# Layer 0's attention sums: the residual on VectorE reads them from PSUM, without ScalarE's copy in SBUF

## The chip, the core and the metric

The kernel runs on one core of a Trainium2 chip. The core has four compute engines and a DMA issuer, each with its own queue of instructions: TensorE (PE, matrix products; PEld is its loading of weights), VectorE (DVE), ScalarE (ACT), GpSimd (POOL) and SyncE (SP, which issues DMAs). [...] TensorE writes its sums to PSUM, a small memory that VectorE and ScalarE also read; everything else lies in SBUF. The metric is the device time of one execution in microseconds (us). All data are float32 unless said otherwise.

## The reference, cut to what matters

Sixteen graphs of 1024 nodes with 256 features pass through four layers, each of the form

```
h = relu(layernorm(x))
x = x + layer(h, adj)
```

Layer 0 is graph attention with its softmax over axis 1, and an ELU at the end:

```
h = input @ W                          # 1024 x 256
e = leaky_relu(f1[:, :, None] + f2[:, None, :], 0.2)
attention = softmax(where(adj > 0, e, NEG_BIG), axis=1)
return elu(attention @ h)
```

Layer 1 is the same with the softmax over the last axis, layer 2 sums over neighbours, divides by the degree and ends in a ReLU, and layer 3 is attention with four heads, a ReLU and a second normalisation. The change concerns only how `elu(s)` with `s = attention @ h` is added to x in layer 0.

## The kernel before, in words

A tile is 128 nodes (the partitions) by 256 features, so a graph has NT = 8 tiles. The kernel computes elu(s) as max(s, 0) + min(exp(s), 1) - 1; the constant -1 per layer is left out of x on the way (the normalisations subtract the mean, and two of them are put back in the row `beta3`, L521). So a tile's end is `x += min(exp(s), 1)` (L736) and `x += max(s, 0)` (L737), two VectorE instructions; L737 also sums the new x along the row into `after.sums`, which the next normalisation needs.

**Layer 0** (L742 to L795), per graph: eight projections (L686, ScalarE evicts them at L746); a row of exponentials sent to all partitions by way of DRAM (L711); eight tiles of attention weights `p` on VectorE (L769, L771), with column sums z by which ScalarE scales the rows of hs (L773); then eight output tiles. Each output tile is a sum of eight products (L759; sixteen matmul instructions, as a float32 product is issued as two) in a PSUM buffer of the pool `at_ps`, which has two buffers. The first EARLY = 2 tiles are summed while the weights are made; tiles 2 to 7 each take the buffer of the tile two before, when that one's last reader is done. Per tile, ScalarE reads the sums twice: `e = exp(s)` (L791) and the copy `v` (L793); then `residual(xs, i, v, after, e)` runs L736 and L737.

**What follows a pair of tiles.** After every second tile `Norm.pair` takes the sums, makes the negative mean `shift` (L635), and ScalarE makes `hn = relu(x + shift)` (L667) and the sum of squares (L640), from which GpSimd makes the inverse deviation (L592, L593). At the next pair `flip` has TensorE transpose hn into PSUM (L680), and ScalarE copies it to `ht` (L681), the input of the next layer's projection.

**Layer 1** ends in the same way, but its `e` and `v` are scaled by 1/z on ScalarE (L838, L840). **Layer 2** has v and no e (L891). Its sums and layer 3's lie in another pool, `hd_ps`. **Layer 3** makes weights p with VectorE (L929), 1278 ns each, and products of 64 weight columns (L942).

**What sets the order.** Each graph is a generator that yields the estimated us of what it has just put down; graph b is due at b x 120, and a loop at the end always goes on with the piece that is due next. So the late layers of one graph are written down between the early layers of the next. The framework then plans each engine's queue from this order, its own estimates of duration, and what is ready and which buffers are free in the plan; it also places all semaphores. Instructions passed to `later(...)` keep the written order on their engine. Among layer 0's outputs of graph b + 1 lie the end of layer 2 and the projection (L906) and first heads of layer 3 of graph b.

Of the kernel before, what the change touches and what calls it, by code (L numbers as in the profile page):

```python
# [8 lines left out]
F32 = mybir.dt.float32  # L9
# [5 lines left out]
P = 128  # L15
# [406 lines left out]
def tile_simple_stack(  # L422
# [11 lines left out]
    nc = tc.nc  # L434
    B, N, D = x.shape
# [32 lines left out]
    work = ctx.enter_context(tc.tile_pool(name="work", bufs=2))  # L468
# [214 lines left out]
    def project(norm, w, n, width):  # L683
        ps = mm_ps.tile([P, HALF], F32, tag="mm", name="ps_proj")
        for c in range(DC):
            nc.tensor.matmul(ps[:, :width], norm.ht[:, c, n * P : (n + 1) * P], w[:, c, :width], start=(c == 0), stop=(c == DC - 1))  # L686
        return ps

    def new_hs(name="hs"):
        return state.tile([P, NT, W3], F32, tag="hs", name=name, bufs=3)  # L690

    def spread(col, n, scales, name):

        k = n * NT
        ps = tr_ps.tile([P, P], F32, tag="tr", name="ps_col")
        nc.tensor.transpose(ps[:k, :], col, ident)
        all_rows = []  # L700
        for scale in scales:
            e = small.tile([H * NT, P], F32, tag="e_row", name="e_row", bufs=2)
            nc.scalar.activation(e[:k, :], ps[:k, :], AF.Exp, scale=scale)
            d = dram.tile([n, N], F32, tag=f"row_{name}", name="d_row", bufs=4)
            later(nc.sync.dma_start(d.rearrange("r (t p) -> (r t) p", p=P), e[:k, :]))
            all_rows += [d[r] for r in range(n)]
        return all_rows

    def everywhere(d, tag):
        row = work.tile([P, N], F32, tag=tag, name="row", bufs=2)  # L710
        later(nc.sync.dma_start(row, d.partition_broadcast(P)))  # L711
        return row

    def column(src, n):

        col = small.tile([P, H, NT], F32, tag="col", name="col", bufs=2)
        nc.vector.tensor_copy(col[:, :n, :], src.rearrange("p t n -> p n t"))
        return col[:, :n, :].rearrange("p n t -> p (n t)")

    def watch(b, layer, terms):  # L720
        k = b * 3 + layer
        nc.vector.tensor_reduce(top[:, k : k + 1], terms, axis=AX.XY, op=OP.max, apply_absolute_value=True)

    def weights(name):
        return work.tile([P, N], F32, tag="p", name=name, bufs=NT)

    def residual(xs, i, v, after, e=None):

        x = xs[:, i, :]
        if i % 2 == 0:  # L730
            if i == NT - 2:
                after.settle()
            after.flip()
            after.sums = small.tile([P, 2], F32, tag="sums", name="sums")
        if e is not None:
            nc.vector.scalar_tensor_tensor(x, e, 1.0, x, op0=OP.min, op1=OP.add)  # L736
        nc.vector.scalar_tensor_tensor(x, v, 0.0, x, op0=OP.max, op1=OP.add, accum_out=after.sums[:, i % 2 : i % 2 + 1])  # L737
        if i % 2:
            after.pair(xs, i // 2, after.sums)


    def layer0(b, xs, m, norm, after):  # L742
        hs = new_hs()
        for n in range(NT):
            ps = project(norm, wx[0], n, D + 2)
            nc.scalar.activation(hs[:, n, : D + 2], ps[:, : D + 2], AF.Copy, scale=norm.rs[n])  # L746
            m.step()
            yield 0.9
        mask = m.bytes
        row_a, row_b = [everywhere(d, "row") for d in spread(column(hs[:, :, D : D + 1], 1), 1, (1.0, S), "l0")]  # L750
        q = small.tile([P, NT], F32, tag="q", name="q")
        nc.scalar.activation(q, hs[:, :, D + 1], AF.Exp, scale=1.0 - S)
        watch(b, 0, hs[:, :, D : D + 2])
        yield 6.38
        ps_ = []
        early = [at_ps.tile([P, HALF], F32, tag="at", name="ps_o0") for _ in range(EARLY)]

        def product(ps, i, j):
            m = nc.tensor.matmul(  # L759
                ps[:, :D], ps_[j][:, i * P : (i + 1) * P], hs[:, j, :D], start=(j == 0), stop=(j == NT - 1)  # L760
            )
            if i < EARLY and j < 7:
                later(m)

        for j in range(NT):
            if m.raws:
                m.step(2)
            p = weights("p0")
            nc.vector.scalar_tensor_tensor(p, row_a, q[:, j : j + 1], row_b, op0=OP.mult, op1=OP.max)  # L769
            z = small.tile([P, 2], F32, tag="z", name="z", bufs=8)  # L770
            nc.vector.scalar_tensor_tensor(p, p, 1.0, mask[:, j, :], op0=OP.mult, op1=OP.mult, accum_out=z[:, 0:1])  # L771
            nc.vector.reciprocal(z[:, 1:2], z[:, 0:1])
            nc.scalar.activation(hs[:, j, :D], hs[:, j, :D], AF.Copy, scale=z[:, 1:2])  # L773
            ps_.append(p)
            if b == 0:
                gates.append(p)
            for i, ps in enumerate(early):
                if j:
                    product(ps, i, j - 1)
            yield 2.6  # L780
        for i, ps in enumerate(early):
            product(ps, i, NT - 1)
        for i in range(NT):
            if i < EARLY:
                ps = early[i]
            else:
                ps = at_ps.tile([P, HALF], F32, tag="at", name="ps_o0")
                for j in range(NT):
                    product(ps, i, j)
            e = work.tile([P, D], F32, tag="e", name="e")  # L790
            nc.scalar.activation(e, ps[:, :D], AF.Exp)  # L791
            v = work.tile([P, D], F32, tag="v", name="v")
            nc.scalar.copy(v, ps[:, :D])  # L793
            residual(xs, i, v, after, e)
            yield 3.9  # L795


# [208 lines left out]
    def graph(b):  # L1006
        xs = loaded.pop(b)
        m = masks.pop(b)
        norm = Norm()
        for g in range(NT // 2):  # L1010
            norm.pair(xs, g)
            m.step()
            yield 2.66
        for layer, inputs in ((layer0, (m,)), (layer1, (m.bytes,)), (layer2, ())):
            yield 2.36
            norm.settle()
            norm.flip()
            after = Norm(degrees(b) if layer is layer1 else None)
            yield from layer(b, xs, *inputs, norm, after)
            norm = after  # L1020
        yield 1.44
        norm.flip()
        res = state.tile([P, NT, H, HW], F32, tag="res", name="res", bufs=1)
        hs = yield from layer3(b, xs, m.bytes, norm, res)
        return tail(b, xs, hs, res)
# [49 lines left out]
    ps = tr_ps.tile([P, P], F32, tag="tr", name="ps_bad")  # L1075
# [64 lines left out]
```

## Time and profile before

Median of 3 runs: 2629.38 us (2628.99 to 2631.85). The profiled execution spans 2618.6 us, with a mean granted TensorE clock of 0.984.

| what | instructions | busy us | mean ns |
|---|---|---|---|
| L759 PE, products of layer 0 | 2048 | 495.6 | 387 |
| L791 ACT, e from PSUM | 128 | 48.6 | 380 |
| L793 ACT, v from PSUM | 128 | 47.2 | 368 |
| L736 DVE, x with e (layers 0 and 1) | 256 | 108.0 | 422 |
| L737 DVE, x with v (layers 0, 1 and 2) | 384 | 160.5 | 421 |
| L737 DVE, reading out the row sum | 384 | 31.1 | 81 |
| L667 ACT, hn in layers 0, 1 and 3's norms | 384 | 176.8 | 500 |
| L929 DVE, p of layer 3 | 512 | 632.9 | 1278 |

How to read the profile: a busy time is that of the engine's own instructions; idle time is put down to the instruction whose semaphore came last before the waiting one began. Instructions of different queues overlap, and neighbours on one queue overlap a little too, as one starts before the other's recorded end. A matmul's recorded duration is longer than its pace, since matmuls are pipelined: L759's follow each other every 0.215 us or so. In the time order a row such as "351.18 2.14 PEld L759 ... x10" merges ten instructions in a row; the first number is the start in us, the second what they took.

### The profile page before, as it was taken

Reading aid. Unit: us, or ns where it says so; the run is one execution under the profiler, and the core shown is the slowest. Engines: PE = TensorE matmul, PEld = TensorE weight load, DVE = VectorE, ACT = ScalarE, POOL = GpSimd, SP = SyncE. Lnnn points to the kernel's source line nnn. Section 1 sums busy time; section 2 is a strip of 40 time slices with the busy share of each in tenths; the row PEclk is TensorE's granted clock in tenths of the full one; section 3 lists DMA queues with packets and bytes.
Section 4 is the critical chain, followed back from the end, with each engine's and each line's share of the span. In section 5 each row is a group of like instructions: output and inputs, shape, how many; then the busy total and the mean of one; then the engine's idle time right before and its main releaser. Section 6 shows DMA issues by size and latency. Waiting matters only on the chain.

```text
span 2618.6 us, 62976 instructions
## 1 busy us (share of the span) xinstructions
PE 2473.6 (94%) x26194; PEld 2100.8 (80%) x26194; DVE 1965.5 (75%) x3815; ACT 1448.0 (55%) x4065; POOL 438.4 (17%) x454
## 2 busy tenths in 40 slices
PE   5899999999999999999999999999999999999985
PEld 4688788888878888788888878888888888878864
DVE  4357778787777877778787777977778787777858
ACT  4564755637565474755637565473755637555350
POOL 1020211203112030211202112030211203111021
PEclk7899999999999999999999999999999999999997
DMA  4531351616217161251616217161351616216021
GB/s 153 117 85 55 93 110 58 125 59 142 66 51 152 65 127 55 91 113 58 125 55 141 70 54 149 66 125 54 99 105 58 125 57 140 70 49 126 26 65 36
DMA packets 212633, 233.76 MB, mean 89 GB/s; under 512 B 10416, under 2 KB 161072, under 8 KB 212336
## 3 DMA queue, kind: packets, MB, share of 16 engines
q0 software_dynamic: 137728, 83.90, 19.4%
q1 hardware_dynamic: 74608, 145.73, 17.1%
q8 instruction: 208, 3.41, 0.5%
q14 instruction: 89, 0.73, 0.1%
HBM read 212.35 MB, written 17.24 MB: 88 GB/s over the span
## 4 chain that ended last, share of the span: by engine, by line
PE 51%; DVE 16%; ACT 15%; DMA 9%; issue 7%; POOL 2%; SPq 0%; DVEq 0%; POOLq 0%; ACTq 0%
PE ps_o L759 16%; PE ps_proj L686 11%; PE ps_o L942 11%; PE ps_o L883 6%; DVE p L929 5%; DVE p L822 4%; ACT hn L667 4%; DMA row<-d_row 3%; DMA raw<-in_adj_t 3%; ACT mask L575 2%; PE pt_h L680 2%; ACT unread L640 2%; PE ps_o L877 2%; PE ps_o L815 2%; POOL rs L593 2%
## 5 line engine op out<-in xcount | busy, mean ns | idle before, releaser
L929 DVE SCALAR_TENSOR_TENSOR p<-row,q,mask 128x1024 f32<-128x1024 f32 x512 | 632.9, 1278 | 60.8 <-PE ps_o L942 51.0
L942 PEld LDWEIGHTS ps_o<-hb,p 128*64 128x64 f32 x16384 | 506.9, 139 | 96.0 <-issue 44.7
L942 PE MATMUL ps_o<-hb,p 128*64 128x65 f32 x16384 | 544.7, 224 | 19.2 <-DVE p L929 6.1
L686 PE MATMUL ps_proj<-wx,ht 128*128 128x258 f32 (+2 forms) x2048 | 517.3, 392 | 6.5 <-ACT hs L746 5.0
L759 PE MATMUL ps_o<-hs,p 128*128 128x256 f32 x2048 | 495.6, 387 | 16.5 <-ACT hs L773 15.9
L815 PE MATMUL ps_o<-hs,p 128*128 128x257 f32 x2048 | 498.1, 390 | 13.0 <-ACT mask L575 7.4
L759 PEld LDWEIGHTS ps_o<-hs,p 128*128 128x128 f32 x2048 | 381.1, 193 | 70.2 <-ACT hs L773 21.5
L815 PEld LDWEIGHTS ps_o<-hs,p 128*128 128x128 f32 x2048 | 374.0, 191 | 69.3 <-ACT mask L575 7.6
L686 PEld LDWEIGHTS ps_proj<-wx,ht 128*128 128x128 f32 x2048 | 360.0, 190 | 85.7 <-ACT hs L746 16.0
L592 POOL TENSOR_SCALAR rs<-mv 128x4 f32<-128x4 f32 (+1 forms) x112 | 33.7, 301 | 1561.4 <-ACT unread L640 1546.8
L736 DVE SCALAR_TENSOR_TENSOR xs<-e,xs 128x256 f32<-128x256 f32 x256 | 108.0, 422 | 237.3 <-ACT e L791 164.0
L593 POOL TENSOR_TENSOR rs<-rs,neg_half 128x4 f32<-128x4 f32 (+2 forms) x144 | 257.3, 1790 | 10.7
L667 ACT ACTIVATE hn<-xs,shift 128x256 f32<-128x256 f32 x384 | 176.8, 500 | 128.3 <-DVE shift L635 126.7
L680 PE MATMUL pt_h<-ident,hn 128*128 128x128 f32 x1024 | 183.6, 285 | 37.9 <-ACT hn L667 36.5
L950 ACT ACTIVATE res<-ps_o 128x260 f32<-128x260 f32 x128 | 48.7, 381 | 298.6 <-PE ps_o L942 298.2
L883 PE MATMUL ps_o<-hi,adj 128*128 128x258 f32 x1024 | 201.2, 320 | 2.4 <-DMA adj<-in_adj 2.3
L680 PEld LDWEIGHTS pt_h<-ident,hn 128*128 128x128 f32 x1024 | 118.3, 141 | 105.6 <-ACT hn L667 85.8
L575 ACT ACTIVATE mask<-raw 128x512 uint8<-128x512 int32 x256 | 160.5, 627 | 71.8 <-DMA raw<-in_adj_t 70.6
L585 POOL DMA_DIRECT2D adj<-in_adj x128 | 114.5, 895 | 486.2 <-PE ps_o L883 452.8
L737 DVE SCALAR_TENSOR_TENSOR xs<-v,xs 128x256 f32<-128x256 f32 x384 | 160.5, 421 | 19.6 <-DVE xs L736 0.5
L769 DVE SCALAR_TENSOR_TENSOR p<-row,q 128x1024 f32<-128x1024 f32 x128 | 159.8, 1269 | 19.7 <-DMA row<-d_row 19.7
L883 PEld LDWEIGHTS ps_o<-hi,adj 128*128 128x128 f32 x1024 | 150.8, 190 | 18.3 <-DMA adj<-in_adj 4.8
(108 smaller groups left out, 3005.4 us busy)
## 6 DMA issues: line engine op xcount, KB each, us to landing
raw<-in_adj_t SPq DMA_DIRECT2D x256, 256.0 KB
adj<-in_adj POOLq DMA_DIRECT2D x128, 512.0 KB, 5.6
row<-d_row SPq DMA_DIRECT2D x112, 512.0 KB
xs<-in_x POOLq DMA_DIRECT2D x32, 512.0 KB, 7.8
out<-xs SPq DMA_DIRECT2D x32, 512.0 KB
wx<-in_w SPq DMA_DIRECT2D x3, 256.0 KB
d_row<-e_row SPq DMA_DIRECT2D x48, 4.0 KB
wts<-in_w_t SPq DMA_DIRECT2D x2, 256.0 KB
```

Source lines behind the costliest of these rows:

```text
L575: nc.scalar.activation(self.bytes[:, n, g * HALF : (g + 1) * HALF], raw, AF.Square, accum_out=squares[:, k : k + 1])
L593: nc.gpsimd.tensor_tensor(rs[:, :n], rs[:, :n], neg_half[:, :n], op=OP.pow)
L667: nc.scalar.activation(hn, xs[:, 2 * g + k, :], AF.Relu, scale=scale, bias=bias)
L680: nc.tensor.transpose(pt[:, c, k * P : (k + 1) * P], hn[:, c * P : (c + 1) * P], ident)
L686: nc.tensor.matmul(ps[:, :width], norm.ht[:, c, n * P : (n + 1) * P], w[:, c, :width], start=(c == 0), stop=(c == DC - 1))
L737: nc.vector.scalar_tensor_tensor(x, v, 0.0, x, op0=OP.max, op1=OP.add, accum_out=after.sums[:, i % 2 : i % 2 + 1])
L759: m = nc.tensor.matmul(ps[:, :D], ps_[j][:, i * P : (i + 1) * P], hs[:, j, :D], start=(j == 0), stop=(j == NT - 1))
L769: nc.vector.scalar_tensor_tensor(p, row_a, q[:, j : j + 1], row_b, op0=OP.mult, op1=OP.max)
L815: nc.tensor.matmul(ps[:, : D + 1], ps_[j][:, i * P : (i + 1) * P], hs[:, j, : D + 1], start=(j == 0), stop=(j == NT - 1))
L883: nc.tensor.matmul(ps[:, : D + 2], adj_n[j][:, i, :], h[:, i, : D + 2], start=False, stop=(h is lo and i == NT - 1), skip_group_check=True,)
L929: nc.vector.scalar_tensor_tensor(p, row, q[:, jj, h : h + 1], mask[:, jj, :], op0=OP.max, op1=OP.mult)
L942: nc.tensor.matmul(pss[g][part, k * HW : (k + 1) * HW], ps_[t][:, i * P : (i + 1) * P][:, part], hbv[:, j + t, h, :], start=(j == 0 and t ...
```

## The change

Layer 0's copy `v` is left out, with its SBUF tile, and `residual` is given the PSUM sums themselves. L737 in layer 0 thus reads x from SBUF and s from PSUM. L736 is as before, and so are layers 1 and 2, whose v is scaled. It is for taking one instruction per output tile, 128 in all, from ScalarE; the last reader of each PSUM buffer of layer 0 is now VectorE's L737 in place of ScalarE's L793.

```diff
             e = work.tile([P, D], F32, tag="e", name="e")
             nc.scalar.activation(e, ps[:, :D], AF.Exp)
-            v = work.tile([P, D], F32, tag="v", name="v")
-            nc.scalar.copy(v, ps[:, :D])
-            residual(xs, i, v, after, e)
+            residual(xs, i, ps[:, :D], after, e)
             yield 3.9
```

## The prediction

> **What bounds the kernel now.** I read the busy shares first, then the windows over one period of the pipeline, then the time order around the changed lines, and last the waits. Busy time of the whole run:
>
> ```profile
> PE 2473.6 (94%) x26194; PEld 2100.8 (80%) x26194; DVE 1965.5 (75%) x3815; ACT 1448.0 (55%) x4065; POOL 438.4 (17%) x454
> ```
>
> TensorE (PE) is nearly always busy, ScalarE (ACT) half the time. A share is a mean over stages, so here is one period of about 157 us, cut at the stages (layer 0's outputs of one graph run from 350 to 382 us):
>
> ```profile
> 350.00:357.80 7.80, 7.78 (x40) 6.12 (x39) 3.91 (x14) 7.32 (x26) 1.22 (x2) 1.00 0.33 62
> 357.80:382.00 24.20, 24.20 (x186) 20.46 (x186) 16.55 (x32) 11.14 (x36) 1.20 (x2) 1.00 0.23 77
> ...
> 430.00:470.00 40.00, 37.60 (x237) 30.38 (x237) 26.63 (x69) 34.26 (x91) 11.83 (x10) 1.00 0.22 67
> ```
>
> The columns after the length are busy us of PE, PEld (weight loads), DVE (VectorE), ACT, POOL. From 357.8 to 382 PE is full and ACT has 13 us to spare; from 430 to 470 ACT is the full engine, but no copy of L793 lies there. Only in the first 7.8 us is ACT tight (94%) where the change acts. Who waits for the copies and for their neighbours (us in total, times, longest):
>
> ```profile
> DVE xs L736 <- ACT e L791: 164.0, 80, 5.7
> ...
> ACT e L791 <- PE ps_o L759: 159.0, 66, 4.2
> ...
> PEld ps_o L759 <- ACT v L793: 0.7, 1, 0.7
> ```
>
> DVE's residual waits for the exponential e, and e for the matmuls. The copy v is hardly waited for: PE once for 0.7 us, and among the releasers of L737 stands v of layer 1 (L840, 0.4 us) but not v of L793. L737 finds v ready because L736 runs while v is copied.
>
> The time order at the start of the outputs, where the first two tiles come together because their sums were built early:
>
> ```profile
> 350.26 0.37 ACT L791 ACTIVATE e<-ps_o 128x256 f32<-128x256 f32 x1
> 350.52 0.36 ACT L793 COPY v<-ps_o 128x256 f32<-128x256 f32 x1
> 350.66 0.42 DVE L736 SCALAR_TENSOR_TENSOR xs<-e,xs 128x256 f32<-128x256 f32 x1 [1.24 <-ACT e L791]
> 351.18 2.14 PEld L759 LDWEIGHTS ps_o<-hs,p 128*128 128x128 f32 x10
> 351.19 0.42 DVE L737 SCALAR_TENSOR_TENSOR xs<-v,xs 128x256 f32<-128x256 f32 x1
> 351.40 2.32 PE L759 MATMUL ps_o<-hs,p 128*128 128x256 f32 x10
> 351.54 0.08 DVE L737 DVE_READ_ACCUMULATOR xs<-v,xs 128x1 f32 x1
> ...
> 353.19 0.91 ACT L667 ACTIVATE hn<-xs,shift 128x256 f32<-128x256 f32 x2 [0.48 <-DVE shift L635]
> ...
> 353.75 0.20 PEld L680 LDWEIGHTS pt_h<-ident,hn 128*128 128x128 f32 x2 [0.43 <-ACT hn L667]
> ```
>
> Read it as: tile 0 is copied by 350.89; its PSUM buffer (one of two) is taken by tile 2's matmuls, whose weights load from 351.18. Then PE loses 0.43 us before L680, which needs hn.
>
> [...] On PSUM the trace has one near pair, the reciprocals, 159 ns from PSUM (L836) and 153 from SBUF (L772): 6 ns, [...] Here e lasts 0.37 from 350.26 and v starts at 350.52, 0.11 of overlap; a dropped copy frees about 0.26 us, not 0.37. [...]
>
> **The change, part by part.**
>
> *Removed: 128 copies on ACT.* Their row says 47.2 us busy (368 ns each); with the overlap about 128 x 0.26 = 33 us of ACT's queue. For the end of the run I cost this at nothing: in the PE-full stage ACT idles anyway, and at 350 to 353 what stands behind the copies (hn at 353.19) waits 0.48 us for DVE's shift, so earlier ACT only waits longer. The DVE chain from e to shift (L736, L737, L893, again L736, L737, L737, L635, from 350.66 to 353.16) has almost no hole that v could have caused.
>
> *Moved: the read of PSUM to L737, 128 times.* [...] I take 30 ns, [...]; 3.8 us in all. In the PE-full stage DVE has 24.2 - 16.6 = 7.6 us spare, which hides it. Only two reads precede the shift at 353.0, so hn comes 0.06 us later [...].
>
> *Added: the buffer is released later.* Before, at the end of v; now at the end of L737's accumulator read. The wait sits on PE's weight load, and all of PE's work queues behind it. I went through the six re-uses of a graph (tile 2 takes tile 0's buffer, up to tile 7). In the steady period five have room: L737 ends 2.2 to 5.2 us before the next weights or matmuls of that buffer, since a tile's 16 matmuls alone take about 3.5 us. (For instance the last re-use: L737 of tile 5 ends at 373.08 and tile 7 starts at 377.74.) The first has none: the release moves from 350.89 to 351.62, plus 0.03 for PSUM and 0.05 for the semaphore (hn ends at 353.70, L680's load starts at 353.75) = 351.70, against a load at 351.18. That is 0.52 us. A load that PE has waited for reaches the multiplier sooner than one queued (the four loads of 350.41 start with their matmuls, those of 351.18 are 0.22 ahead), so about 0.1 comes back: PE stalls some 0.4 us. What absorbs it: the 0.43 us at L680. Ten matmuls at 0.215 from 351.40 are over at 353.56; hn's transposes get going at about 353.85; so 0.29 of the 0.4 is time PE would have lost there. Net 0.11 us, and from there PE is full up to 403 us, so it stays. The same times stand in 14 of the 16 graphs. Graph 1 has 0.5 us more room before the first re-use: 0.2. Graph 0, alone at the start, has none (copy ends 59.65, load follows, L737 ends at 60.38): 0.85, and nothing absorbs it that I can see.
>
> Sum: 14 x 0.11 + 0.2 + 0.85 = 2.6 us. Before 2629.4, so 2632.0.
>
> **Rivals.** *A, the stall is paid in full.* If hn comes later too (it hangs on both reads), the wait at L680 does not shrink: 14 x (0.4 + 0.06) + 1.05 = 7.5 us, 2636.9; [...]. For it: 350 to 357 is tight on ACT and PE both. Against: hn's delay is a few hundredths, and the 0.43 is there in the rows.
>
> *B, faster.* The order on each queue is planned anew from estimated costs, since one ACT instruction a tile goes and the buffer's release moves. In 350 to 357.8 three copies (350.52, 351.82, 357.51) leave, 0.8 us of 7.8; if the plan lets hn or layer 3's projection L686 come forward so that the 0.43 us vanishes in 15 graphs, the gain is 6.5 us: 2622.9. For it: ACT's 94% there. Against: hn waits for DVE, not for ACT, and that chain gets longer.
>
> *C, clearly slower.* DVE's plan puts a p of L929 (1278 ns) ahead of a residual that now holds a buffer. At 376.99 it does so already, between L736 and L737 of tile 6, where nothing needs the buffer soon. If that befell one tight re-use a graph: 16 x 1.28 = 20 us, 2650. Against: at 350 to 357 layer 3's weights aren't yet being made.
>
> **How the numbers follow.** My forecast (same within 0.2%, that is within 5.3 us, near 2632): 0.42. A: 0.25. B: 0.24. C: 0.09. A and C are slower, 0.34; B faster, 0.24. Range: B's 2622.9 may be outdone where L686's wait of 0.36 us before 350.41 shrinks too (0.25 x 15 = 3.8), so 2619; [...].
>
> **What would show it.** Right: L793 gone; [...] a new wait of PE's weight loads L759 for DVE L737, some 0.4 us once a graph; the wait of L680 for hn shorter by 0.2 to 0.3 at that place; L736 still waiting about 164 us for e; ACT's busy time down by 47. Wrong: tile 2's matmuls put behind other PE work, a stall in more than one re-use, or a period that differs by more than 0.3 us from 157 with PE's order changed in stages that hold no layer 0 output.

## The result, and the profile after

The change made the kernel slower: 2642.86 us, median of 4 runs (2635.77 to 2645.67), against 2629.32 us before; the ratio is 1.0045 with a 95% interval of 1.0023 to 1.0067. The loss is small, about 0.45%, but clear of the noise. A second measurement, beside other kernels, gave 1.0047 (1.0032 to 1.0063). ScalarE lost its 128 copies, and nothing was gained by it. The line of busy times of the changed kernel:

```profile
PE 2479.5 (94%) x26194; PEld 2101.2 (80%) x26194; DVE 1969.2 (75%) x3815; ACT 1419.8 (54%) x3937; POOL 438.6 (17%) x454
```

ACT is busy 28 us less with 128 instructions fewer; the other engines' busy times are within 6 us of those before. So most of the lost time is idle time. The start of layer 0's outputs and the rest of them, in the same graph as before (windows that begin and end at the same work, to within 0.1 us; columns as before):

```profile
350.78:359.29 8.51, 7.95 (x40) 6.47 (x39) 4.34 (x14) 7.76 (x25) 1.23 (x2) 1.00 0.30 56
359.29:383.34 24.05, 24.05 (x184) 20.29 (x184) 15.58 (x29) 9.06 (x27) 1.20 (x2) 1.00 0.25 78
```

The first stretch takes 8.5 us for the forty matmuls that took 7.8, and PE idles 0.56 us in it; the second is full as it was. Who waits (us in total, times, longest):

```profile
ACT e L791 <- PE ps_o L759: 174.9, 67, 4.5
DVE xs L736 <- ACT e L791: 124.1, 64, 5.4
...
PEld pt_h L680 <- ACT hn L667: 100.0, 176, 2.4
...
DVE hb L911 <- ACT hs L904: 61.1, 48, 3.6
```

Before, the last two were 85.8 and 22.3 us (line numbers after the change are two lower from layer 1 on: L904 was L906, L911 was L913). What grew are TensorE's waits for hn and VectorE's for the evicted projection of layer 3 (hb is made from it). L737 as an end of TensorE's waits, which I had forecast once in every graph, is hardly there; the rows of L737 by what it reads (min, median, max in ns), and who waited for it:

```profile
L737 DVE SCALAR_TENSOR_TENSOR xs<-v,xs x256: 403/420/429, 120.8 to 2553.4; 128x256 f32<-128x256 f32 x128
...
L737 DVE SCALAR_TENSOR_TENSOR xs<-ps_o,xs x128: 415/424/426, 60.5 to 2444.1; 128x256 f32<-128x256 f32 x128
...
  PEld ps_o L759: 1.4, 1
```

The 420 is that of layers 1 and 2. In layer 0 itself L737 is no slower: for tiles 2 to 7 of the graph shown its median is 425 ns before, with both operands in SBUF, and 424 now, with one in PSUM; over all 128 the means are 423.2 and 423.4. So the read of PSUM costs nothing that these traces show. Then what fills the first stretch? The time order of the changed kernel:

```profile
348.02 0.47 ACT L889 ACTIVATE v<-ps_o,z 128x256 f32<-128x256 f32 x1 [2.44 <-PE ps_o L881]
...
350.23 0.73 PEld L759 LDWEIGHTS ps_o<-hs,p 128*128 128x128 f32 x4 [0.42 <-ACT hs L773]
...
351.04 0.38 ACT L791 ACTIVATE e<-ps_o 128x256 f32<-128x256 f32 x1
...
351.36 0.92 ACT L667 ACTIVATE hn<-xs,shift 128x256 f32<-128x256 f32 x2
...
351.91 0.42 DVE L737 SCALAR_TENSOR_TENSOR xs<-ps_o,xs 128x256 f32<-128x256 f32 x1
351.93 0.20 PEld L680 LDWEIGHTS pt_h<-ident,hn 128*128 128x128 f32 x2 [0.96 <-ACT hn L667]
351.93 0.84 PE L680 MATMUL pt_h<-ident,hn 128*128 128x128 f32 x4 [0.56 <-ACT hn L667]
352.17 0.50 ACT L640 ACTIVATE unread<-xs,shift 128x256 uint8<-128x256 f32 x1
352.26 0.08 DVE L737 DVE_READ_ACCUMULATOR xs<-ps_o,xs 128x1 f32 x1
...
352.49 3.32 PEld L759 LDWEIGHTS ps_o<-hs,p 128*128 128x128 f32 x16
...
353.88 0.50 ACT L904 ACTIVATE hs<-ps_proj,rs 128x264 f32<-128x264 f32 x1
```

And the rows of before that stood at these places:

```profile
349.89 0.47 ACT L906 ACTIVATE hs<-ps_proj,rs 128x264 f32<-128x264 f32 x1
...
350.41 0.74 PEld L686 LDWEIGHTS ps_proj<-wx,ht 128*128 128x128 f32 x4 [0.36 <-ACT hs L906]
...
350.78 0.49 ACT L891 ACTIVATE v<-ps_o,z 128x256 f32<-128x256 f32 x1
```

The queues have another order. Before, layer 2's last v (L891) came after e of tile 0, and the first eviction of layer 3's projection (L906) ahead of it; that eviction freed a projection buffer, and TensorE had four matmuls of L686 to do while tile 0's sums were read. Now layer 2's last v comes 3 us ahead of e, hn follows e, and the first eviction comes 2.8 us after e. TensorE has nothing to do after tile 1's last product but transposes that wait for hn, and its loads idle 0.96 us, its products 0.56. Tile 2's products stand behind the transposes.

Matched instruction by instruction over a period, TensorE's work has the order of before except here and for two L686 at the end of the period. Taken from the last four products of tiles 0 and 1, the matmuls behind the first stretch come 0.69 us later than before (median of 14 graphs). Another 0.19 us is lost just ahead: the loads of those four products wait 0.42 us for hs (L773; the row at 350.23), which ScalarE now runs behind layer 2's last v, and before they did not wait. Fifteen graphs at 0.88 are an estimate of 13 us, against 11.8 that the ratio means. Whole periods are too rough for this. Their mean over 14 graphs is 157.13 us before and 158.43 and 157.84 in the two traces of the changed kernel. But it is 157.66 in a kernel of experiment 1 below that runs TensorE in the order of before and hardly loses time.

### The profile page after: what moved, and what is told of

Read it like the earlier page. It is cut to its first block, busy times and chain, and to the rows that moved or that the text cites. A ratio compares the mean times of both kernels' runs of the same rounds, so it can differ in the third digit from the quotient of the medians.

```text
span 2639.1 us, 62745 instructions
## 1 busy us (share of the span) xinstructions
PE 2479.5 (94%) x26194; PEld 2101.2 (80%) x26194; DVE 1969.2 (75%) x3815; ACT 1419.8 (54%) x3937; POOL 438.6 (17%) x454
## 4 chain that ended last, share of the span: by engine, by line
PE 47%; ACT 17%; DVE 14%; DMA 12%; issue 7%; POOL 2%; SPq 0%; DVEq 0%; POOLq 0%; ACTq 0%
PE ps_o L759 14%; PE ps_o L940 11%; PE ps_proj L686 10%; PE ps_o L881 5%; DVE p L927 5%; DMA row<-d_row 4%; ACT hn L667 4%; DVE p L820 4%; DMA raw<-in_adj_t 3%; ACT unread L640 3%; ACT mask L575 3%; PE pt_h L680 2%; PE ps_o L813 2%; PE ps_o L875 2%; ACT ht L681 2%
## 5 line engine op out<-in xcount | busy, mean ns | idle before, releaser
L686 PE MATMUL ps_proj<-wx,ht 128*128 128x258 f32 (+2 forms) x2048 | 512.1, 391 | 7.1 <-ACT hs L746 5.0
L759 PE MATMUL ps_o<-hs,p 128*128 128x256 f32 x2048 | 491.5, 387 | 17.6 <-ACT hs L773 16.5
L759 PEld LDWEIGHTS ps_o<-hs,p 128*128 128x128 f32 x2048 | 380.3, 192 | 76.6 <-ACT hs L773 27.3
L686 PEld LDWEIGHTS ps_proj<-wx,ht 128*128 128x128 f32 x2048 | 362.4, 190 | 84.1 <-ACT hs L746 16.2
L736 DVE SCALAR_TENSOR_TENSOR xs<-e,xs 128x256 f32<-128x256 f32 x256 | 108.1, 422 | 206.0 <-ACT e L791 124.1
L680 PE MATMUL pt_h<-ident,hn 128*128 128x128 f32 x1024 | 181.9, 286 | 48.6 <-ACT hn L667 46.7
L680 PEld LDWEIGHTS pt_h<-ident,hn 128*128 128x128 f32 x1024 | 116.3, 141 | 117.5 <-ACT hn L667 100.0
L881 PE MATMUL ps_o<-lo,adj 128*128 128x258 f32 x1024 | 163.6, 293 | 0.0
```

The lines of the kernel that those rows point to most:

```text
L680: nc.tensor.transpose(pt[:, c, k * P : (k + 1) * P], hn[:, c * P : (c + 1) * P], ident)
L759: m = nc.tensor.matmul(ps[:, :D], ps_[j][:, i * P : (i + 1) * P], hs[:, j, :D], start=(j == 0), stop=(j == NT - 1))
L881: nc.tensor.matmul(ps[:, : D + 2], adj_n[j][:, i, :], h[:, i, : D + 2], start=False, stop=(h is lo and i == NT - 1), skip_group_check=True,)
```

## The experiments

Three theories. **P, the plan**: what the copy of tile 0 did for the planned order is the cause. **H, the hold**: TensorE waits for a buffer that VectorE holds. **S, spread**: each of the eight reads of a graph costs its share. All ratios are to the kernel before, measured beside it on the same chip. It took 2629.57 us beside experiments 1 to 3 and 2624.97 beside 4 and 5, so times of the two groups are compared by their ratios.

**1. Which tile's copy matters?** First only tile 0 is read direct, that is, from PSUM without the copy; then all tiles but tile 0:

```diff
+            v = ps[:, :D]
+            if i != 0:        # the second kernel: if i == 0
-            v = work.tile([P, D], F32, tag="v", name="v")
-            nc.scalar.copy(v, ps[:, :D])
+                v = work.tile([P, D], F32, tag="v", name="v")
+                nc.scalar.copy(v, ps[:, :D])
```

> Only tile 0 of each graph's eight is read from PSUM by the residual; tiles 1 to 7 keep ScalarE's copy. Theory P (plan): without tile 0's copy ScalarE's planned queue runs the next norm's hn first, and TensorE's planned queue puts the transposes L680, which wait for hn, ahead of tile 2's products; this costs about 0.7 us a graph, so the whole loss comes back: ratio to before 1.003 to 1.006, 2638 to 2645 us. Theory H (hold): TensorE waits for the buffer that VectorE holds; tile 0's is the tight one, so nearly the whole loss as well. Theory S (spread): each of the eight reads costs its share on the engines' chains: an eighth, 1.0006, near 2631 us.

Measured: 2644.25 us, 1.0068 (1.0053 to 1.0083).

> The copy is kept for tile 0 alone; tiles 1 to 7 are read from PSUM. Theories P and H: TensorE's order is as before and tile 0's buffer is released as before: ratio 0.998 to 1.001, 2625 to 2632 us. Theory S: seven eighths of the loss, ratio 1.004, about 2640 us.

Measured: 2630.45 us, 1.0008 (1.0000 to 1.0016). Sixteen copies of 128 make the whole loss; leaving out the other 112 costs at most 0.16%, and brings nothing. S is out. With tile 0 alone direct, the order of TensorE's 26194 matmuls is that of the changed kernel throughout, and with all but tile 0 it is, but for 4 places, that of the kernel before.

**2. The copy made, but not read.** VectorE reads PSUM and ScalarE copies as before:

```diff
             nc.scalar.copy(v, ps[:, :D])
-            residual(xs, i, v, after, e)
+            residual(xs, i, ps[:, :D], after, e)
```

> VectorE reads PSUM for all tiles, and ScalarE still makes the copy, which nothing reads. Theory P: ScalarE's queue is filled as before and so TensorE's planned order is much like before, with the buffer held by VectorE: at most the stall, ratio 1.000 to 1.002, 2629 to 2635 us. Theory H: the buffer is released as late as in the changed kernel: the full loss, 1.003 to 1.006, and a wait of L759's weight loads for L737 in nearly every graph. Theory S: VectorE's reads cost the same: 1.004.

Measured: 2633.95 us, 1.0015 (1.0000 to 1.0029). Here the stall of the prediction can be seen. Weight loads, and the total of that wait:

```profile
350.99 0.74 PEld L686 LDWEIGHTS ps_proj<-wx,ht 128*128 128x128 f32 x4 [0.36 <-ACT hs L906]
352.26 2.02 PEld L759 LDWEIGHTS ps_o<-hs,p 128*128 128x128 f32 x10 [0.53 <-DVE xs L737]
```

```profile
PEld ps_o L759 <- DVE xs L737: 9.6, 16, 1.4
```

The loads of tile 2 wait 0.53 us for L737 here, and about as long once in each of graphs 2 to 15, where I had worked out 0.52. (The other two of the 16 waits are in graph 0.) Four matmuls of L686 run ahead of it as before. The products start 0.27 us later than before, and are 0.22 later at the end of the stretch: 15 x 0.22 = 3.3 us, near the measured 0.15% (3.9 us). So the hold is real, but it is about a third of the loss, and the interval reaches down to nothing.

**3. No copy, and the buffer free early.** L737 is given e, and layer 0's sums are left out of its output:

```diff
-            v = work.tile([P, D], F32, tag="v", name="v")
-            nc.scalar.copy(v, ps[:, :D])
-            residual(xs, i, v, after, e)
+            residual(xs, i, e, after, e)
```

> L737 is given e in place of the sums, so layer 0's output is max(e, 0) + min(e, 1): it leaves out the sums themselves, and no copy is made. The buffer is released at the end of e, earlier than before. Theory P: ScalarE's queue lacks the copies as in the changed kernel, and the order on TensorE is like the changed kernel's: loss of 1.003 to 1.006, 2637 to 2645 us. Theory H: no buffer is held, no loss: 0.997 to 1.000. Theory S, as far as VectorE's PSUM reads are its cause: no loss.

Measured: 2633.41 us, 1.0017 (1.0007 to 1.0026). P expected the full loss and H none; both are wrong. The evictions come late as in the changed kernel (VectorE's hb waits 52.2 us for them), but the plan could put four of tile 2's products ahead of the transposes:

```profile
352.54 2.37 PE L759 MATMUL ps_o<-hs,p 128*128 128x256 f32 x8
354.74 0.60 PE L680 MATMUL pt_h<-ident,hn 128*128 128x128 f32 x4
355.18 0.60 PE L759 MATMUL ps_o<-hs,p 128*128 128x256 f32 x2
```

Eight of L759 in a row, where the changed kernel has four and then the wait: the last four are tile 2's, whose buffer is free at the end of e. So the new order of ScalarE's queue doesn't bring the full loss by itself: it also matters that tile 2's buffer is not free when the plan looks for work to put ahead of the transposes.

**4. What re-ordered ScalarE's queue?** Not only ScalarE's time can be the link. The v of layers 0, 1 and 2 are tiles of one tag in the pool `work`, which has two buffers for it. By the order in which the tiles are asked for, tile 0's v stands ahead of layer 2's last v for a buffer (the traces leave buffer numbers out, so this is read from the code). Theory **L**: that slot set the order; theory **A**: ScalarE's freed 0.26 us did. This kernel has no copies at all, but takes the slot for tile 0 by one column that GpSimd writes:

```diff
+            if i == 0:
+                v = work.tile([P, D], F32, tag="v", name="v")
+                nc.gpsimd.tensor_copy(v[:, :1], e[:, :1])
+            residual(xs, i, ps[:, :D], after, e)
```

> All eight tiles are read from PSUM, no copy on ScalarE; for tile 0 a tile of the pool slot of v is still taken, and GpSimd puts one column of e into it, which nothing reads. Theory L (slot): what the copy of tile 0 did for the plan was to hold one of the two buffers of v, behind which layer 2's last v had to wait; with the buffer held TensorE's order is like that of the run with the unread copy: ratio 1.000 to 1.003, 2629 to 2637 us, first eviction L906-alike ahead of e of tile 0. Theory A (ScalarE's time): the missing 0.26 us of ScalarE re-ordered its queue; the loss of the changed kernel stays: 1.004 to 1.007.

Measured: 2631.29 us, 1.0022 (1.0015 to 1.0030), and beside it the changed kernel once more:

> The changed kernel as it is, beside the others on one chip: 1.0045 before with an interval of 1.0023 to 1.0067; if its planned order on TensorE, which equals that of the kernel with only tile 0 direct, decides the time, 1.005 to 1.008, 2641 to 2650 us.

Measured: 2636.85 us, 1.0047 (1.0032 to 1.0063), a little under what I had expected. ScalarE's order with the slot held:

```profile
349.91 0.47 ACT L907 ACTIVATE hs<-ps_proj,rs 128x264 f32<-128x264 f32 x1
350.28 0.71 ACT L791 ACTIVATE e<-ps_o 128x256 f32<-128x256 f32 x2
350.89 0.47 ACT L892 ACTIVATE v<-ps_o,z 128x256 f32<-128x256 f32 x1
```

The first eviction is ahead of e again and layer 2's v behind it, without any copy on ScalarE, and the wait of VectorE's hb for evictions is 21.6 us. L's forecast came and A's did not. The same was seen in 15 graphs of every trace: wherever tile 0 takes the slot, layer 2's last v runs behind tile 0's e, and wherever it doesn't, ahead of it. What no run separates is the slot from GpSimd's small extra instruction, which takes it here and also reads e. How the planner gets from the earlier place of that v to the later eviction isn't shown either.

The rest, 0.22%, I put down to the later release of the buffer, but by the plan and not by a wait. Tile 0's buffer is free at 351.79, and L759's loads wait for L737 only twice in the whole run. TensorE's queue has six L686 ahead of tile 2 where four stood before, and the last two wait for an eviction:

```profile
351.85 0.30 PEld L686 LDWEIGHTS ps_proj<-wx,ht 128*128 128x128 f32 x2 [0.67 <-ACT hs L907]
352.18 0.84 PEld L759 LDWEIGHTS ps_o<-hs,p 128*128 128x128 f32 x4
```

Tile 2's first product comes 0.90 us later after e than before, of which 0.29 is left at the end of the stretch.

**5. Taking the second condition away as well.** In layer 0 VectorE does the max with the sums first and the min with e second (with the row sum), so that the buffer is free one instruction earlier; alone, and with the slot held as in 4:

```diff
+            nc.vector.scalar_tensor_tensor(x, v, 0.0, x, op0=OP.max, op1=OP.add)
+            nc.vector.scalar_tensor_tensor(x, e, 1.0, x, op0=OP.min, op1=OP.add, accum_out=total)
```

> As the changed kernel, but VectorE does the max with the sums first and the min with e second, with the row sum read out there, so the PSUM buffer is free about 0.45 us earlier. Theory L with the held buffer as second condition: layer 2's last v still comes early and TensorE still has only transposes to wait for, for about 0.4 us less: 1.002 to 1.005. If the held buffer had no part, as the changed kernel: 1.004 to 1.007.

Measured: 2637.64 us, 1.0049 (1.0035 to 1.0062): no better than the changed kernel. This lies within both forecasts, so the run doesn't decide between them. In its trace two transposes, still waiting 0.56 us for hn, come ahead of tile 2's products, and the stretch ends 0.51 us late:

```profile
351.52 1.13 PE L764 MATMUL ps_o<-hs,p 128*128 128x256 f32 x4
353.22 0.44 PE L680 MATMUL pt_h<-ident,hn 128*128 128x128 f32 x2 [0.56 <-ACT hn L667]
```

The four of L764 (L759 in this kernel's numbering) end tiles 0 and 1. As long as TensorE's next piece in the plan is hn's transposes, an earlier buffer is worth little.

> The two together: max first, and the slot of v taken for tile 0 by a column that GpSimd writes. Theory L: the order before e of tile 0 is as in the kernel before, and the buffer comes free in time for tile 2: 0.997 to 1.001, 2622 to 2632 us. Theory A: ScalarE's queue still lacks the copies: 1.003 or more.

Measured: 2624.59 us against 2624.97 of the kernel before, 0.9993 (0.9984 to 1.0003). TensorE's row at that place is unbroken, L686 and then fourteen of L764:

```profile
351.95 1.16 PE L686 MATMUL ps_proj<-wx,ht 128*128 128x264 f32 x4
352.94 3.19 PE L764 MATMUL ps_o<-hs,p 128*128 128x256 f32 x14
```

All 128 copies are gone here and the loss with them; no version beat the kernel before by more than its interval. The cases side by side:

| | buffer free before L737 would free it | buffer held to the end of L737 |
|---|---|---|
| layer 2's last v behind e (slot taken) | 1 (before); all but tile 0: 1.0008; max first: 0.9993 | unread copy 1.0015; slot by GpSimd 1.0022 |
| layer 2's last v early (slot free) | e for v: 1.0017; max first: 1.0049 | 1.0045 and 1.0047 (the change); tile 0 alone 1.0068 |

Do the lost pieces add up to the times? For each kernel the table adds what TensorE's matmuls lose in the first stretch and just ahead of it (medians of 14 graphs, each matched with the kernel before). An estimate of 15 such graphs lies within the interval of every ratio:

| kernel | lost per graph, us | 15 of these as a ratio | measured |
|---|---|---|---|
| the change | 0.69 + 0.19 | 1.0050 | 1.0045, 1.0047 |
| tile 0 alone direct | 0.86 + 0.19 | 1.0060 | 1.0068 |
| max first | 0.51 + 0.19 | 1.0040 | 1.0049 |
| e for v | 0.10 + 0.19 | 1.0017 | 1.0017 |
| slot by GpSimd | 0.29 | 1.0017 | 1.0022 |
| unread copy | 0.22 | 1.0013 | 1.0015 |
| all but tile 0 | 0.00 | 1.0000 | 1.0008 |
| max first, slot taken | -0.15 | 0.9991 | 0.9993 |

The 0.19 stands in exactly the four kernels whose layer 2's last v runs early. Tile 0 alone direct has the changed kernel's order on TensorE, but its first eviction comes 3.10 us after e, not 2.84; whether its time is really worse is not settled, as the intervals overlap.

A kernel in which layer 0's copies have buffers of their own, the plainest test of the slot, was not run. Single periods of 160 to 162 us, with a late row of layer 3 (VectorE's p waits for a DMA), stand in the traces of several of these kernels, the changed one among them, so single traces differ by more than the medians do.

## Why the prediction was right or wrong

The time, 2642.9, lies inside the recorded range (2619 to 2643) by 0.1 us, and that is luck: the likeliest case, no change near 2632, did not come, and none of the cases behind the range describes what happened. The range's top rested on my estimate of a read of PSUM, which was not shown. "Slower" had 0.34.

- *The copies cost nothing to remove.* Right for ScalarE's time: 112 copies fewer, 1.0008. Wrong for what else a copy holds (by experiment 4 a slot, with GpSimd's instruction as the rival left). I followed the copy's time on its queue and who waited for its data; I did not ask which pool slot its output took, and who was planned behind that. This is the step that failed: "For the end of the run I cost this at nothing" holds for the copy's time, but tile 0's sixteen copies held the order in which layer 2's last v comes late, and without them TensorE loses 0.69 us a graph at tile 2 and 0.19 ahead of it. Rival B had the new planning in it, but only as a gain, and C only with a p of layer 3 in front.
- *The buffer of the first re-use is released too late, by 0.52 us.* Right where the order stayed: 0.52 to 0.57 in graphs 2 to 15 of the run with the unread copy. In the changed kernel tile 2's loads stand behind the transposes, and L737 is done before their turn. The other five re-uses of these graphs had room, as forecast: none of them waited for L737 in that run.
- *The wait at L680 absorbs 0.29 of it, 0.11 is left.* Mis-sized: 0.22 was left with the unread copy. The loads' waits for hn in that stretch did shrink, from 0.65 to 0.22 us in most graphs, but of the 0.27 us by which tile 2 started late only 0.05 came back. The rows of transposes and products were also cut in another way than before, so the waits are not the same waits.
- *A read of PSUM costs 30 ns.* That was my estimate, and no trace showed it: the one near pair of before differs by 6 ns. In layer 0 L737's mean is 423.4 ns where it was 423.2 before, so the read plays no part. The 0.06 us by which hn was to come later and 0.03 of the 0.52 rested on the 30 ns.
- *What would show it wrong* named tile 2's matmuls behind other TensorE work, and that is what happened. Two signs of being right failed as well: L736 waits 124.1 us for e, not 164, and ACT's busy time is down by 28 us, not 47 (the working itself had 33, with the overlap). Rival A's 2636.9 would be a ratio of 1.0029, inside the first interval of the change (1.0023 to 1.0067) and just under the second (1.0032 to 1.0063), but by another way: its stall for L737 is hardly in the changed kernel's trace.
- *From 430 to 470 ACT is the full engine* is misread: in the row shown PE is busy 37.6 of 40 us and ACT 34.3. Nothing else in the working rests on it.

## What to carry to other kernels

An instruction that is removed takes more than its time with it: its output held a slot, and where a planner fills the queues by what is free, as here, a slot that comes free early can pull another layer's work ahead and push off what kept the full engine fed. Before calling a removed instruction free, list the buffers it took and who shares them, and look at what the full engine runs during the next wait. Here one tile in eight made the whole loss; trying the change on one tile at a time found it in two runs.

## What the runs showed of the hardware

VectorE's 128x256 float32 instruction L737 took 423.4 ns (mean of 128) in layer 0 of the changed kernel, with one operand in PSUM, and 423.2 in layer 0 of the kernel before, with both in SBUF. A wait of a weight load is not a loss of the same size: with the unread copy tile 2's loads waited 0.52 us for VectorE's reader in most graphs, and the products were 0.22 us late at the end of the stretch. ScalarE's time was worth little in this kernel: with all but tile 0 direct 112 of its 128 copies are gone, and the time is 1.0008 of before (1.0000 to 1.0016).
